# A graph-attention and hypergraph kernel: the order of the first three pairs

## The chip, the core and the metric

The kernel runs on one core of a Trainium2 chip. A core has a matrix engine (TensorE, PE in the profile), three engines for element work (VectorE or DVE, ScalarE or ACT, GpSimd or POOL) and a queue engine (SyncE or SP) that issues transfers. All of them run their own instruction streams in order and wait for each other by semaphores. SBUF is the working memory with 128 partitions; PSUM, in eight banks of 512 floats per partition, is where TensorE writes. The metric is the device time of one execution in microseconds; lower is better.

## The reference

`x` has 128 graphs of 128 nodes with 512 features, `adj` a 0/1 matrix for each graph. Layer 0 is graph attention with 8 heads of 64 units, then a residual and a layer norm. Layer 1 is two hypergraph convolutions with a ReLU and a layer norm between them, then two residuals and a layer norm. All is float32.

```python
# layer 0, per graph
feats = einsum('nf,hfu->hnu', X, W)
e_self, e_neigh = feats @ a_self, feats @ a_neigh            # per head and node
dense = leaky_relu(e_self[:, :, None] + e_neigh[:, None, :], 0.2)
dense = dense + -1e10 * (1 - A)
att = softmax(dense, axis=-1)
x = layernorm(x + relu(einsum('hij,hju->ihu', att, feats) + b))
# layer 1, per graph; hypergraph_conv(x, W) is
H = (adj != 0); w = adj[0]                                   # w: the first row
Dn = 1 / sum_e(H * w); Be = 1 / sum_n(H)
conv = Dn * (H @ (Be * (H.T @ (x @ W.T)))) + b
h = layer_norm(relu(conv(x, W1, b1)), gamma, beta)           # 512 -> 1024
y = conv(h, W2, b2) + x                                      # 1024 -> 512
out = layernorm(x + y)
```

## The kernel before, in words

The graphs are handled in 64 pairs. A pair passes through some five stages, and the stages of successive pairs overlap as in a pipeline. The program is written out without loops on the chip: every piece of work is a Python function, and `todo` holds each with a due time (`T` = 38.6 per pair and lag). Sorting by due time gives the order of the instructions on every engine's stream. The table `first` (L1161) gives single pieces of single pairs another due time; only the first pairs are in it. The times set an order and nothing else.

Stages of a pair, with the lines of the profile:

- Loads: `a` and the first row `w` (L106, L112), the rows `x` (L120), the rows in blocks `xb` (L129), the adjacency in blocks `ab` (L137). From pair 2 on, `x_transpose` (L385) turns `xb` on VectorE into `xT`; pairs 0 and 1 are turned on TensorE (L397).
- `nodes` (L360 to L369) makes the node degrees on VectorE; they go out to memory and come back spread over the partitions (`write_nodes`, `spread_nodes`, L374, L576). `edges` (L421 to L428) makes the edge degrees, `scale_edges` (L435) scales by them, `propagator` (`pd`) multiplies them and `r_evict` (L451) makes `R`, the propagation matrix.
- Features: for pairs 0 and 1 plain products (L523); from pair 2 on, seven half-size products in the manner of Strassen (`pfX`, `pfY`, `pfW`), with sums of operands on GpSimd (`x_sums`, L469), copies on ScalarE (L344) and sums of results on VectorE (`f_sum`, L509). The same seven products stand for the first weights (`ph`) and the second (`py`); `y_sum` (L935) adds the latter's results.
- Scores: `spread_rows` (L542) writes the per-node terms to memory, `neighbours` (L570) loads them to all partitions as `nb`. In four groups (two graphs, two halves of the heads): `masked` adds the mask (GpSimd, L589), `leaky` is the leaky ReLU with the own term (ScalarE, L605; one group of pair 0 on VectorE, L598), `largest` the maximum (VectorE, L611), `exponential` (ScalarE, L619).
- The exponentials must stand the other way round. For pair 0 TensorE turns them (L651). From pair 1 on they are written to memory (L623), read back in blocks (L631) and turned on VectorE in blocks (L640) into `eT`.
- Attention: products with `eT` (`pav`; L677 for pair 0, L703 for others, where the last head of both graphs shares a third bank), division (`attended`, L714, L735), residual and moments (L751, L759), reciprocal deviation (`rsa` on GpSimd from `vea`, L765 to L767), scaling on ScalarE (L794).
- Layer 1: `propagate` (`pz`), its copy (L829) and sums (L840), the hidden products, sums (L866), ReLU (L881), squares (L892), their tree of sums (`squares`, GpSimd, L904). For all but the last pairs the sums cross the partitions by a trip through memory: `sum_blocks` (L950 to L955), `write_sums` (L960), `read_sums` (L965), `sum_rest` (L973). From them `rsh` (L1002) and the scaling `y_scale` (L1006), then the output product `pq`, the last norm and the store.

The weights are prepared while the first pairs run: the attention vectors are folded into W0 (L230 to L238); `prepare_hidden` (L249) makes sums of W1 blocks; `prepare_output` (L276) multiplies gamma and beta through W2, its row sums are copied (L284) and spread (`gw`, `bw`, L288), and `prepare_output_blocks` (L300) rescales W2 by them in 16 instructions, after which the block sums follow (L226).

PSUM banks come in turn from one ring of eight. Transfers go out on SP's queue in program order, and a few early ones on ScalarE's; a transfer also waits until the one issued eight earlier on the same semaphore has landed.

Of the kernel before, what the change touches and what calls it, by code (L numbers as in the profile page):

```python
# [20 lines left out]
def kernel(  # L21
# [167 lines left out]
    load_adj(1)  # L189
# [61 lines left out]
    gbs = const.tile([P, KH, 2], F32, name="gbs")  # L251
# [13 lines left out]
    def prepare_rows():  # L265

        made["sel"] = work.tile([2, 2, P], F32, tag="zT", name="sel")
        nc.gpsimd.tensor_copy(
            made["sel"], ident[:2, :2].unsqueeze(2).to_broadcast([2, 2, P])
        )  # L270

    def prepare_output():
        pv = made["pv"] = [bank(f"pv{j}") for j in range(2)]
        for blk, i, j in w2_blocks:
            for k in range(KH // 2):
                nc.tensor.matmul(  # L276
                    pv[j][:2, :QU], gbs[:, i * KH // 2 + k, :], blk[:, k, :],
                    start=(i == 0 and k == 0), stop=(i == 1 and k == KH // 2 - 1),
                )

    def prepare_output_sums():
        made["sums"] = const.tile([2, F], F32, name="sums")
        for j in range(2):
            nc.vector.tensor_copy(made["sums"][:, j * QU:(j + 1) * QU], made["pv"][j][:2, :QU])  # L284
# [41 lines left out]
    def chain(kind, lag, times, multiply, w, extra=0, since=0, until=PAIRS):  # L326

        tag = "chain" if w == HALF else "half"

        def product(p, s, i):
            where, start = {1: ("X", 1), 2: ("Y", 1), 6: ("X", 0), 5: ("W", 1), 7: ("X", 0),
                            4: ("X", 0), 3: ("W", 0)}[i]
            if start:
                s[kind, where] = bank(f"{kind}{where}_{p}")
            multiply(s, i, s[kind, where], start)

        def copy(p, s, i):
            n = w + (extra if i < 2 else 0)
            t = s[kind, i] = work.tile([P, HALF if w == HALF else FW], F32, tag=f"{tag}_{i}", name=f"{kind}{i}_{p}")
            nc.scalar.copy(t[:, :n], s[kind, "X"][:, :n])  # L344

        for i, t in zip((1, 2, 6, 5, 7, 4, 3), times):
            at(lag, t, product, i, since=since, until=until)
        for i, t in enumerate(times[7:]):
            at(lag, t, copy, i, since=since, until=until)
# [166 lines left out]
    def plain_features(p, s, i):  # L516
        if i == 0:
            s["pf"] = [[bank(f"pf_{p}_{g}{j}") for j in range(2)] for g in range(2)]
        for j in range(2):
            w = (w0_sb[:, 0], w0_12, w0_sb[:, 1], w0_sb[:, 2])[2 * i + j]  # L520
            for g in range(2):
                for k in range(KF // 2):
                    nc.tensor.matmul(  # L523
                        s["pf"][g][j][:, :FW], s["xT"][:, g, i * KF // 2 + k, :],
                        w[:, k].rearrange("p h u -> p (h u)"), start=(i == 0 and k == 0),
                        stop=(i == 1 and k == KF // 2 - 1), skip_group_check=True,
                    )

    def plain_features_out(p, s):
        s["ft"] = fts[p]  # L530
        for j in range(2):
            for g in range(2):
                (nc.vector.tensor_copy if g or p else nc.scalar.copy)(  # L533
                    s["ft"][:, g, j * HH:(j + 1) * HH, :UW], by_head(s["pf"][g][j])
                )

    @step(1, 25.0)
    def spread_rows(p, s):


        rows = work.tile([P, B], F32, tag="rows", name=f"rows_{p}")
        nc.vector.transpose(  # L542
            rows.rearrange("p (c x) -> p c x", c=2),
            s["ft"][:, :, :, :2].rearrange("p g h c -> p c (g h)"),
        )
        shape = [B, NB, B] if p == 0 else [NB, B, B]
        rd = s["rd"] = dram.tile(shape, F32, tag="rd", name=f"rd_{p}")
        if p == 0:
            for b in range(NB):
                (nc.sync, nc.scalar)[b % 2].dma_start(rd[:, b, :], rows[b * B:(b + 1) * B])  # L550
        else:
            nc.sync.dma_start(rd.rearrange("b c j -> (b c) j"), rows)

    def blocked(p, t):

        dims = "p (h b j) -> p b h j" if p == 0 else "p (b h j) -> p b h j"
        return t.rearrange(dims, b=NB, h=H)

    @step(1, 27.0)
    def neighbours(p, s):  # L560
        s["nb"] = work.tile([P, 2, H * N], F32, tag="nb", name=f"nb_{p}")
        for g in range(2):
            dst, src, hs = s["nb"][:, g, :], s["rd"], slice((2 + g) * H, (3 + g) * H)
            if p == 0:
# [80 lines left out]
    def e_transpose_first(p, s, g, q):  # L645
        if (g, q) == (0, 0):
            s["eT"] = work.tile([P, 2, H, N], F32, tag="eT", name=f"eT_{p}")
        t = bank(f"pet_{g}{q}")
        for h in range(HH):
            n = (q * HH + h) * N  # L650
            nc.tensor.transpose(t[:, h * N:(h + 1) * N], s["nb"][:, g, n:n + N], ident)  # L651
        (nc.scalar.copy if q else nc.vector.tensor_copy)(
# [3 lines left out]
    for (g, q), tm, (lag, tl), (lagx, tx), te, tt in (  # L656
# [7 lines left out]
        at(2, tt, e_transpose, g, q, since=1)  # L664

    for g in range(2):
        at(2, (6.2, 10.9)[g], e_write, g, since=1)
        at(2, (10.0, 14.9)[g], e_read, g, since=1)
# [19 lines left out]
    @step(2, 20.9, since=1, until=LAST)  # L688
    def attend_rest(p, s):
        s["pav", 2] = bank(f"pav_{p}_2")  # L690

    @step(2, 24.1, since=1, until=LAST)
    def attend_pair(p, s):

        rest = s["pav", 2][:, :2 * (U + 1)].rearrange("p (g u) -> p g u", g=2)
        to = [(rest[:, g, :], g, HB) for g in range(2)]
        for g in range(2):
            t = s["pav", g] = bank(f"pav_{p}_{g}")
            to += [(t[:, h * (U + 1):(h + 1) * (U + 1)], g, h) for h in range(HB)]
        for t, g, h in to:  # L700
# [23 lines left out]
    def attended_pair(p, s):  # L724
# [4 lines left out]
        for r, t, dst in [(rden[:, :, HB], rest, heads[:, :, HB, :])] + [  # L729
# [3 lines left out]
        ]:  # L733
# [388 lines left out]
    for t, fn, *args in (  # L1122
# [17 lines left out]
        (12.1, load_weights, (nc.scalar, w2_blocks, w2t, DH // 2, QU)),  # L1140
        (13.05, prepare_vectors, ()),
        (14.05, load_weights, (nc.scalar, w1_blocks[:2], w1t, F // 2, HALF)),
        (12.95, load_first_row, (1,)),
        (15.46, load_weights, (nc.sync, w1_blocks[:1:-1], w1t, F // 2, HALF)),
        (16.1, everywhere, (b2_bc, b2, nc.sync)),
        (79.0, prepare_hidden, (nc.gpsimd, 0)), (79.1, prepare_hidden, (nc.gpsimd, 1)),
        (120.7, prepare_hidden, (nc.gpsimd, 2)), (110.6, prepare_hidden, (nc.vector, 3)),
        (15.5, prepare_output_vectors, ()), (16.0, prepare_output, ()),
        (78.3, prepare_rows, ()), (78.79, prepare_output_sums, ()),
        (78.99, prepare_output_spread, (0, "gw")), (98.0, prepare_output_spread, (1, "bw")),  # L1150
        (98.1, prepare_output_bias, ()), (98.2, prepare_output_blocks, (slice(0, 1),)),
        (99.75, prepare_output_blocks, (slice(1, 2),)),
        (117.8, prepare_output_blocks, (slice(2, 3),)),
        (118.1, prepare_output_blocks, (slice(3, 4),)),
        (126.5, prepare_output_block_sums, (nc.gpsimd, slice(0, 2))),
        (126.57, prepare_output_block_sums, (nc.vector, slice(2, 3))),
        (141.0, prepare_output_block_sums, (nc.vector, slice(3, 4))),
# [3 lines left out]
    first = {  # L1161
        ("spread_rows", 0): 13.5, ("neighbours", 0): 14.0,
        ("nodes", 0): 12.9, ("write_nodes", 0): 12.92, ("spread_nodes", 0): 15.9,
        ("edges", 0): 14.46, ("edges", 2): 119.2,
        ("x_transpose", 2, 0): 120.5, ("x_transpose", 2, 1): 121.1, ("scale_edges", 0): 14.47, ("propagator", 0): 14.55,
        ("r_evict", 0): 97.845,
        ("spread_rows", 1): 15.72, ("nodes", 1): 15.55, ("write_nodes", 1): 15.85,
        ("edges", 1): 110.4, ("scale_edges", 1): 110.5, ("neighbours", 1): 80.1,
        ("propagator", 1): 121.7, ("spread_nodes", 1): 80.3, ("r_evict", 1): 121.8,
        ("leaky", 0, 1, 1): 77.65, ("leaky", 0, 0, 1): 73.6, ("largest", 0, 0, 1): 75.3,  # L1170
# [4 lines left out]
        ("leaky", 1, 0, 0): 113.0, ("leaky", 1, 0, 1): 117.9, ("leaky", 1, 1, 0): 119.9,  # L1175
        ("largest", 1, 0, 0): 113.1, ("largest", 1, 0, 1): 118.2, ("largest", 1, 1, 0): 120.2,
        ("masked", 1, 0, 0): 98.0, ("masked", 1, 0, 1): 98.1, ("masked", 1, 1, 0): 98.2, ("masked", 1, 1, 1): 120.65,
        ("exponential", 1, 0, 0): 119.85, ("exponential", 1, 1, 1): 126.6,
        ("square", 0, 0, 0): 134.5, ("square", 0, 0, 1): 134.6,
        ("mask", 3): 152.0, ("sum_blocks", 0): 149.75, ("write_sums", 0): 149.76,  # L1180
        ("read_sums", 0): 149.77,
        ("squares", 0, 0, 0): 141.3, ("squares", 0, 0, 1): 141.4, ("squares", 0, 0, 2): 141.5,
        ("nodes", 2): 149.8, ("write_nodes", 2): 149.9, ("spread_nodes", 2): 150.3,
        ("r_evict", 2): 160.4,
        ("nodes", 3): 154.6, ("write_nodes", 3): 154.7, ("skip", 0): 132.5,
# [5 lines left out]
    for p, time, fn, *args in (  # L1191
# [3 lines left out]
        (0, 13.0, plain_features_out), (1, 13.1, x_transpose_out, 0), (1, 13.8, x_transpose_out, 1),  # L1195
        (1, 14.5, plain_features, 0), (1, 14.6, plain_features, 1),
        (1, 15.6, plain_features_out), (1, 97.9, adj_transpose_first),
        (0, 78.8, e_transpose_first, 0, 0), (0, 78.85, e_transpose_first, 0, 1),
        (0, 78.9, e_transpose_first, 1, 0), (0, 78.93, e_transpose_first, 1, 1),
    ):  # L1200
        todo.append((time, run, (fn, p, args)))
    for p in range(PAIRS):
        if p > 1:
            todo.append(({2: 79.5, 3: 143.1}.get(p, p * T), load, (p,)))
            todo.append((16.2 if p == 2 else p * T + (19.0 if p == 3 else 2.0), load_blocks, (p,)))
            todo.append((p * T + (28.5 if p == 2 else 20.5), load_edges, (p,)))
        for lag, time, name, pairs, fn, args in steps:
# [11 lines left out]
            if p == LAST - 1:  # L1219
                time = {  # L1220
                    ("product", 2): 24.22 if (lag, time) > (3, 20.0) else time,
                    ("product", 5): 29.5 if (lag, time) > (3, 20.0) else time,
# [53 lines left out]
```

## Time and profile before

| | us |
|---|---|
| median of 3 runs | 2405.86 (2405.43 to 2407.07) |
| the profiled execution | 2395.3 |
| its span | 2393.4 |
| mean granted TensorE clock | 0.996 |

The profile is of one execution. Its rows show one engine each: start, duration, engine, line, operation, result<-operands, shapes, count, and in brackets how long the engine was idle before and what ended that. Busy times of TensorE overlap, since products are pipelined: the step from one start to the next is what a product costs. Waits are put down to the releaser that came last.

Stretch by stretch, busy times in us:

| stretch | PE | DVE | ACT | POOL |
|---|---|---|---|---|
| 0 to 50 | 37.05 | 34.81 | 20.66 | 24.93 |
| 50 to 100 | 45.21 | 48.74 | 31.50 | 41.54 |
| 100 to 155 | 52.66 | 48.14 | 35.04 | 40.17 |
| 155 to 210 | 55.00 | 45.92 | 34.34 | 43.75 |

### The profile page before, as it was taken

Reading aid. Unit: us, or ns where it says so; the run is one execution under the profiler, and the core shown is the slowest. Engines: PE = TensorE matmul, PEld = TensorE weight load, DVE = VectorE, ACT = ScalarE, POOL = GpSimd, SP = SyncE. Lnnn points to the kernel's source line nnn. Section 1 sums busy time; section 2 is a strip of 40 time slices with the busy share of each in tenths; the row PEclk is TensorE's granted clock in tenths of the full one; section 3 lists DMA queues with packets and bytes.
Section 4 is the critical chain, followed back from the end, with each engine's and each line's share of the span. In section 5 each row is a group of like instructions: output and inputs, shape, how many; then the busy total and the mean of one; then the engine's idle time right before and its main releaser. Section 6 shows DMA issues by size and latency. Waiting matters only on the chain.

```text
span 2393.4 us, 80729 instructions
## 1 busy us (share of the span) xinstructions
PE 2360.8 (99%) x32309; PEld 2026.8 (85%) x32309; DVE 2089.6 (87%) x4456; ACT 1528.5 (64%) x4481; POOL 1825.6 (76%) x2060
## 2 busy tenths in 40 slices
PE   7899999999999999999999999999999999999998
PEld 6788887888888888888888888888888888888886
DVE  7989888898898898898898888988988988988975
ACT  4565765756667667667667666666676676676662
POOL 5877786777877877877877778778778778778774
PEclk9999999999999999999999999999999999999999
DMA  6555454555554555555545555544545555555541
GB/s 197 133 148 150 143 144 134 159 143 147 151 148 144 149 148 148 151 143 154 144 142 157 141 147 155 146 146 147 150 143 153 147 150 139 148 156 140 149 128 37
DMA packets 431134, 347.09 MB, mean 145 GB/s; under 512 B 151440, under 2 KB 380328, under 8 KB 430760
## 3 DMA queue, kind: packets, MB, share of 16 engines
q1 hardware_dynamic: 427288, 337.46, 49.5%
q8 instruction: 256, 4.19, 0.7%
q10 hardware_dynamic: 3472, 4.47, 0.6%
q14 instruction: 118, 0.97, 0.2%
HBM read 239.08 MB, written 102.73 MB: 143 GB/s over the span
## 4 chain that ended last, share of the span: by engine, by line
PE 89%; DMA 4%; DVE 3%; ACT 1%; POOL 1%; issue 1%; SPq 1%; DVEq 0%; POOLq 0%; ACTq 0%
PE phX L97 17%; PE pyX L97 17%; PE pfX L97 8%; PE pyW L97 8%; PE phW L97 8%; PE pav L703 5%; PE phY L97 4%; PE pz L97 4%; PE pfW L97 4%; PE pq L97 4%; PE pyY L97 4%; PE pfY L97 2%; DMA ed<-nb 1%; PE pd L97 1%; DMA nb<-rd 1%
## 5 line engine op out<-in xcount | busy, mean ns | idle before, releaser
L344 ACT COPY py<-pyX 128x257 f32<-128x257 f32 x189 | 70.7, 374 | 538.5 <-PE pyX L97 465.6
L97 PEld LDWEIGHTS phX<-zS,w_sb 128*64 128x64 f32 x6144 | 350.6, 137 | 36.3 <-POOL ft L742 23.1
L97 PE MATMUL phX<-zS,w_sb 128*64 128x128 f32 x6144 | 373.4, 273 | 2.6 <-ACT ph L344 2.6
L904 POOL TENSOR_TENSOR sq<-sq 128x512 f32<-128x512 f32 (+2 forms) x384 | 343.9, 896 | 20.1
L589 POOL TENSOR_TENSOR nb<-nb,neg 128x512 f32<-128x512 f32 x256 | 319.9, 1284 | 23.1 <-DMA nb<-rd 12.7
L605 ACT ACTIVATE nb<-nb,ft 128x128 f32<-128x128 f32 x1020 | 325.1, 392 | 13.7 <-POOL nb L589 13.7
L619 ACT ACTIVATE nb<-nb,nm 128x128 f32<-128x128 f32 x1024 | 319.4, 392 | 4.2 <-DVE nm L611 4.0
L767 POOL TENSOR_TENSOR rso<-veo,mhalf 128x2 f32<-128x2 f32 x63 | 44.2, 701 | 338.4 <-DVE veo L765 338.4
L97 PE MATMUL pyX<-w_sb,hS 128*64 128x257 f32 x2016 | 245.1, 380 | 0.0
L97 PE MATMUL pyX<-w_sb,h 128*64 128x257 f32 x2016 | 243.7, 379 | 0.5 <-ACT py L344 0.5
L97 PE MATMUL pyW<-w_sb,hS 128*64 128x256 f32 x2016 | 243.3, 378 | 0.0
L881 ACT ACTIVATE h<-h,vecs 128x128 f32<-128x128 f32 x768 | 239.4, 394 | 2.0 <-DVE h L866 1.4
L611 DVE TENSOR_REDUCE nm<-nb 128x4 f32<-128x512 f32 x256 | 175.2, 684 | 48.8 <-ACT nb L605 46.2
L97 PEld LDWEIGHTS pyX<-w_sb,h 128*64 128x64 f32 x2016 | 173.7, 136 | 46.2 <-ACT py L344 0.9
L97 PEld LDWEIGHTS pyW<-w_sb,hS 128*64 128x64 f32 x2016 | 174.7, 136 | 43.6 <-issue 0.3
L742 POOL TENSOR_TENSOR ft<-ft,b_bc 128x512 f32<-128x512 f32 x128 | 203.9, 1613 | 6.1 <-ACT ft L533 6.1
L97 PEld LDWEIGHTS pyX<-w_sb,hS 128*64 128x64 f32 x2016 | 168.7, 137 | 38.7 <-issue 0.8
L640 DVE STREAM_TRANSPOSE eT<-eb 128x512 f32<-128x512 f32 x252 | 163.5, 685 | 5.7 <-DMA eb<-ed 4.7
L805 DVE SCALAR_TENSOR_TENSOR o<-y,b_bc 128x512 f32<-128x512 f32 x128 | 164.7, 1325 | 0.0
L1006 DVE SCALAR_TENSOR_TENSOR y<-y,rsh,bw_bc 128x512 f32<-128x512 f32 x126 | 150.1, 1229 | 14.9 <-POOL rsh L1002 14.9
L469 POOL TENSOR_TENSOR hS<-h 128x512 f32<-128x512 f32 x126 | 162.1, 1287 | 0.0
L892 ACT ACTIVATE sq<-h 128x512 f32<-128x512 f32 x256 | 160.6, 629 | 2.1
(178 smaller groups left out, 5672.4 us busy)
## 6 DMA issues: line engine op xcount, KB each, us to landing
nb<-rd SPq DMA_DIRECT2D x127, 512.0 KB, 5.6
ed<-nb SPq DMA_DIRECT2D x126, 512.0 KB, 3.4
eb<-ed SPq DMA_DIRECT2D x504, 128.0 KB, 2.9
x<-in_x_dram SPq DMA_DIRECT2D x64, 512.0 KB, 4.0
out_dram<-o SPq DMA_DIRECT2D x63, 512.0 KB, 2.9
xb<-in_x_dram SPq DMA_DIRECT2D x248, 128.0 KB, 5.5
a<-in_adj_dram SPq DMA_DIRECT2D x64, 128.0 KB, 2.4
w<-in_adj_dram SPq DMA_DIRECT2D x128, 64.0 KB, 5.0
```

What stands on the lines that cost most here:

```text
L97: nc.tensor.matmul(to[rows], lhs[:, rows], rhs, start=start, stop=stop, skip_group_check=True)
L469: engine.tensor_tensor(t[:, i], in0, in1, op=op)
L589: nc.gpsimd.tensor_tensor(t, t, neg[:, :, None, :].to_broadcast([P, NB, HH, B]), op=ALU.add)
L605: nc.scalar.activation(t, t, AF.Prelu, bias=s["ft"][:, g, h, 0:1], alpha=SLOPE)
L611: nc.vector.tensor_reduce(s["nm"][:, g, hs], scores(p, s, g, hs).rearrange("p b h j -> p h b j"), AX.XY, ALU.max, negate=True,)
L619: nc.scalar.activation(t, t, AF.Exp, bias=s["nm"][:, g, h:h + 1])
L640: nc.vector.transpose(s["eT"][:, g, hs, :].rearrange("p h (b i) -> p h b i", b=NB), s["eb", g][:, :, hs, :].rearrange("p b h j -> p h b j"),)
L742: nc.gpsimd.tensor_tensor(t, t, b0_bc.rearrange("p (h u) -> p h u", h=H), op=ALU.add)
L805: nc.vector.scalar_tensor_tensor(s["o"][:, g, :], s["y"][:, g, :], 2.0, b2_bc, op0=ALU.mult, op1=ALU.add)
L881: nc.scalar.activation(dst[:, k, :], src[:, k, :], AF.Relu, bias=b1_sb[:, c:c + 1])
L892: nc.scalar.activation(s["sq"][:, g, q * KH // 2:(q + 1) * KH // 2, :], hid(s, g, q), AF.Square, scale=DH ** -0.5,)
L904: nc.gpsimd.tensor_tensor(t[:, :n, :], t[:, :n, :], t[:, n:2 * n, :], op=ALU.add)
```

## The change

Due times of pairs 0 to 3 are moved, and some pieces are done in another way:

- Pair 2's features run around pair 0's propagation: five products before it and two after it. Its rows are loaded and turned early, and its row terms are sent early.
- Pair 1's exponentials are turned on TensorE, as pair 0's; their trip through memory is dropped, and pair 1's score terms lie head by head as pair 0's.
- For pair 0, leaky comes ahead of the mask.
- In `attend_pair` the heads run in order (graph 0, graph 1, each with its last head at its end), and `attended_pair` reads in that order.
- Pair 1's plain features run one half of the columns after the other.
- `prepare_output` makes 32 result rows at a time in one bank in place of 2 rows in two banks; the sums are then copied and spread over 128 partitions.
- Loads are regrouped: two of four W2 blocks and pair 1's adjacency go behind pair 0's neighbour terms, pair 1's first rows far later.
- Nodes, edges, squares, sums and preparations of the first pairs stand elsewhere in the queues.

```diff
-    load_adj(1)
-    gbs = const.tile([P, KH, 2], F32, name="gbs")
+    gbs = work.tile([P, KH, B], F32, tag="y", name="gbs")
+    nc.gpsimd.memset(gbs, 0.0)
+    one = small.tile([P, 2], F32, tag="one", name="one", bufs=1)
+    nc.vector.tensor_reduce(
+        one, ident.rearrange("p (c r) -> p r c", c=NB)[:, :2], AX.X, ALU.add
+    )
...
     def prepare_output():
-        pv = made["pv"] = [bank(f"pv{j}") for j in range(2)]
...
+        t = made["pv"] = bank("pv")
+        for n in range(2):
+            for j in range(2):
+                for c in range(NB):
+                    k = 2 * c + n
+                    blk = w2_blocks[2 * (k // (KH // 2)) + j][0]
+                    nc.tensor.matmul(
+                        t[c * B:(c + 1) * B, j * QU:(j + 1) * QU], gbs[:, k, :],
+                        blk[:, k % (KH // 2), :], start=(n == 0 and j == 0), stop=(n == 1),
+                        skip_group_check=True,
+                    )
...
-        at(2, tt, e_transpose, g, q, since=1)
+        at(2, tt, e_transpose, g, q, since=2)
...
-        at(2, (6.2, 10.9)[g], e_write, g, since=1)
-        at(2, (10.0, 14.9)[g], e_read, g, since=1)
+        at(2, (6.2, 10.9)[g], e_write, g, since=2)
+        at(2, (10.0, 14.9)[g], e_read, g, since=2)
...
     def attend_rest(p, s):
-        s["pav", 2] = bank(f"pav_{p}_2")
+        s["pav", 0] = bank(f"pav_{p}_0")
...
+        s["pav", 1], s["pav", 2] = (bank(f"pav_{p}_{g}") for g in (1, 2))
         rest = s["pav", 2][:, :2 * (U + 1)].rearrange("p (g u) -> p g u", g=2)
-        to = [(rest[:, g, :], g, HB) for g in range(2)]
+        to = []
         for g in range(2):
-            t = s["pav", g] = bank(f"pav_{p}_{g}")
+            t = s["pav", g]
             to += [(t[:, h * (U + 1):(h + 1) * (U + 1)], g, h) for h in range(HB)]
+            to.append((rest[:, g, :], g, HB))
...
-        (12.1, load_weights, (nc.scalar, w2_blocks, w2t, DH // 2, QU)),
+        (12.1, load_weights, (nc.scalar, w2_blocks[:2], w2t, DH // 2, QU)),
+        (14.03, load_weights, (nc.sync, w2_blocks[2:3], w2t, DH // 2, QU)),
+        (14.04, load_weights, (nc.scalar, w2_blocks[3:], w2t, DH // 2, QU)),
+        (14.045, load_adj, (1,)),
-        (12.95, load_first_row, (1,)),
+        (80.2, load_first_row, (1,)),
...
+        ("edges", 3): 157.0,
+        ("write_nodes", 3): 158.6,
+        ("nodes", 3): 158.5,
+        ("nodes", 2): 144.25,
+        ("read_sums", 0): 152.22,
+        ("sum_blocks", 0): 152.2,
+        ("squares", 0, 1, 2): 151.5,
+        ("squares", 0, 1, 1): 151.4,
+        ("squares", 0, 1, 0): 151.3,
+        ("nodes", 1): 121.72,
+        ("x_transpose", 2, 1): 78.1,
+        ("x_transpose", 2, 0): 75.4,
+        ("leaky", 0, 1, 1): 15.61,
+        ("leaky", 0, 1, 0): 69.62,
+        ("leaky", 0, 0, 1): 69.61,
+        ("leaky", 0, 0, 0): 69.6,
+        ("edges", 2): 144.21, ("scale_edges", 2): 144.22,
+        ("pf_product", 2, 1): 78.991, ("pf_copy", 2, 0): 78.9915, ("pf_product", 2, 2): 78.992,
+        ("r_evict", 1): 144.23,
...
+        (1, 124.95, e_transpose_first, 0, 0), (1, 124.96, e_transpose_first, 0, 1),
+        (1, 130.41, e_transpose_first, 1, 0), (1, 130.42, e_transpose_first, 1, 1),
...
-            todo.append((16.2 if p == 2 else p * T + (19.0 if p == 3 else 2.0), load_blocks, (p,)))
-            todo.append((p * T + (28.5 if p == 2 else 20.5), load_edges, (p,)))
+            todo.append(({2: 11.05, 3: 105.8}.get(p, p * T + 2.0), load_blocks, (p,)))
+            todo.append(({2: 105.7, 3: 146.85}.get(p, p * T + 20.5), load_edges, (p,)))
```

## The prediction

> **What bounds the kernel now.** I read the busy times of the page first, then TensorE's waits, then each engine's timeline of the first 170 us.
>
> ```profile
> PE 2360.8 (99%) x32309; PEld 2026.8 (85%) x32309; DVE 2089.6 (87%) x4456; ACT 1528.5 (64%) x4481; POOL 1825.6 (76%) x2060
> ```
>
> TensorE is busy nearly all the time. Its timeline far into the run shows one pair's propagation start and the next's:
>
> ```profile
> 1008.67 1.95 PE L97 MATMUL pz<-R,y 128*64 128x128 f32 x32
> ...
> 1045.04 1.95 PE L97 MATMUL pz<-R,y 128*64 128x128 f32 x32
> ```
>
> A pair costs 36.37 us, with no gap between rows. So from about 155 us to the tail only TensorE counts, and a change to the first pairs moves the end by what it moves TensorE's arrival there. TensorE's waits, longest in total first (us, times, longest):
>
> ```profile
> PE px L397 <- DMA x<-in_x_dram: 8.1, 1, 8.1
> PE pz L97 <- ACT y L794: 4.0, 1, 4.0
> PE pav L703 <- DVE eT L640: 4.0, 2, 2.3
> PE phX L97 <- ACT ph L344: 2.6, 2, 1.9
> PE phX L97 <- ACT zT L829: 1.3, 2, 0.9
> PE pfX L97 <- ACT pf L344: 1.2, 2, 0.7
> ```
>
> Past the first load, about 11 us of gaps lie in the start-up. Its landmarks, from the TensorE timeline (start, duration, and in brackets the gap before):
>
> ```profile
> 29.72 1.89 PE L276 MATMUL pv<-w_sb,gbs 128*2 128x256 f32 x8
> ...
> 47.23 3.68 PE L97 MATMUL pz<-R,y 128*64 128x128 f32 x32 [4.05 <-ACT y L794]
> ...
> 87.06 1.94 PE L97 MATMUL pz<-R,y 128*64 128x128 f32 x32
> ...
> 101.26 1.92 PE L97 MATMUL pq<-y,R 128*64 128x512 f32 x8
> ...
> 116.62 1.97 PE L703 MATMUL pav<-ft,eT 128*64 128x65 f32 x60 [1.72 <-DVE eT L640]
> ```
>
> Pair 0's propagation starts at 47.23, pair 1's at 87.06, pair 2's attention products end at 118.59. Busy time by stretch says what bounds the stretch: VectorE was busy 48.7 of 50 us from 50 to 100, TensorE 45.2. The start-up is bound by VectorE, in queue order. VectorE's timeline shows pair 2's node degrees stretched:
>
> ```profile
> 86.63 1.36 DVE L360 SCALAR_TENSOR_TENSOR w<-a,w 128x128 f32<-128x128 f32 x1
> ...
> 88.03 1.12 DVE L365 TENSOR_SCALAR dn<-dd 128x2 f32<-128x2 f32 x1
> ...
> 105.08 0.28 DVE L360 SCALAR_TENSOR_TENSOR w<-a,w 128x128 f32<-128x128 f32 x1
> ```
>
> The set took 4.4 us beside GpSimd's masks (86.14 to 90.54), 1.35 us with GpSimd idle (105.08). Last, the sync queue: the round trip of the square sums, and the write of pair 2's exponentials.
>
> ```profile
> 86.24 0.33 SPq L960 DMA_DIRECT2D sd<-sr  x1
> 89.41 0.63 SPq L965 DMA_DIRECT2D sums_out<-sd  x1
> ...
> 98.68 1.43 SPq L623 DMA_DIRECT2D ed<-nb  x1
> ```
>
> **What the Trainium skill says.** "SBUF — State Buffer", Who interferes with whom: a VectorE instruction with two SBUF inputs, or in a two-port mode, and a GpSimd instruction that reads SBUF block each other for the whole instruction. The 4.4 against 1.35 us agrees. "TensorE: Matmul & The Clock Gate", What's actually happening: after some 3.4 us idle the array runs at half rate. Agrees: after the 4.05 us gap, propagation took 3.46 us start to start (47.23 to 50.69), pair 1's 1.75. "TensorEngine Tiling (Array Packing)", Theoretical Speedup: products of 32 output columns can run up to four at once. The trace shows two at once for 64 columns (a 264-wide record takes 0.11 us of TensorE, 8 in 0.89, against 0.233 at full width, 16 in 3.73), not four. "DMA: Bandwidth & Descriptors", Anatomy of one DMA: about 2 us fixed. The square sums' write took some 3.1 us here (86.24 to 89.41).
>
> **The change, part by part,** in times of this execution.
>
> *To pair 0's normalization.* Before, ScalarE starts at 29.24, after the first mask, and runs 3.73 + 4.77 us without a hole to 37.64. With leaky first it starts at the landing, 27.95: leaky to 31.7, masks behind it (1.27 each) to 34.2, exponentials 31.7 to 36.65, held 0.2 by a maximum that stands behind a turn of pair 2's rows (1.06). That is 1.0 us; with the transposes and copies of that step, vea comes at 44.0 instead of 45.16. The weight product pv is 32 records of 256 columns: 7.0 us now, 1.7 if four run at once. Two W2 blocks now load behind pair 0's neighbour rows. Those and W1 moved 3.2 MB from 24 to 35.7, 273 GB/s, so the blocks land near 31.5, pv ends near 33.3, before the transposes need TensorE. If not four at once, pv ends at 38.5 and all that follows is 1.5 to 2 us later. The last W1 block lands 1.2 MB / 273 = 4.2 us later, near 39.9; behind it on SP stand pair 1's row writes and neighbour loads, which land near 45, as now (no engine waited for them at 45.92). Cover about 1 us.
>
> *The gap at 43.18.* Pair 2's features, 7 x 0.89 us, move here from 64.9 to 74.4; four and a fifth fill 40 to 45.4. Propagation starts near 45.9, at full rate, ends 47.7 instead of 50.7; two more products follow, and the hidden layer starts at 49.5 instead of 50.69. Later TensorE no longer spends 6.2 us plus 1.2 us of gaps on these, but 1.9 us on pair 1's transposes and 0.9 on bw. Its own bound for pair 1's propagation is then 82, 5 us earlier than 87.06.
>
> *VectorE's queue.* Same operations, other order. From vea_0 44.0: a hold of 2.3 us, because the second feature sum stands behind the ScalarE copy that follows y (46.95); then by their spacing in this trace 0.7 + 6.3 (16 W2 rescales at 0.39) + 2.4 (maxima) + 1.1 + 1.8 (hidden sums) + 1.4 (nodes of pair 1, out of 25.7) + 1.5 (edges) + 2.6 (four PSUM copies for four turns of 0.65) + 1.3 + 0.5 + 1.8 + 0.2 = 21.6, to 67.9. Contended: half of the 3 us seen for nodes, 0.9 for the rest; waits for pair 1's last leaky and hidden sum, 1.1: 71.4. Attended to vea_1 takes 5.9 (78.51 to 84.42): 77.3. Before: 84.4.
>
> *What is late next.* Between vea_1 and the y sum that frees pyW now stand: a W2 sum 1.06, edges of pair 2 2.0, its scaling 0.5, R 0.33, nodes 1.36. That is 5.3 us clear, 11.3 at the worst this trace shows for each (2.15, 2.5, 1.9, 0.33, 4.4); GpSimd's masks and squares run just then, so I take 8.3. The two sums, 0.7: 86.3. The last weighing product (1.7) is queued behind them: pair 1's propagation at 88.0, against 87.06. The 5 us are spent: +0.9, bounds -2 and +4.
>
> *To pair 2's attention.* GpSimd's second squares move behind the masks: ready near 87. A turn, a maximum and the block sums on VectorE (1.05, 0.6, 1.0): 89.0. The round trip (sd issue to readable, 5.7 us from 86.24 and 89.41 plus a like landing) ends at 94.7, and VectorE now stands waiting there some 3 us; before, it came at 96.18 without a wait. Behind it: sums 0.5, maximum 0.6, edges 1.9, nodes 2.9, so 100.6. Then h sum, two scalings and R, 2.9: output product at 103.5 (101.26 before). SP writes pair 2's exponentials after those nodes: 101.1 (98.68 before). The chain from that write to the turned second group took 16.5 us before (115.17), so 117.6. TensorE gets there at 103.5 + 13.2 (101.26 to 114.58, less its gaps) + 0.7 for ScalarE's copy = 117.4. With heads in order, group 0 (0.95 us) runs while group 1 is turned, to 118.35: end 119.4 against 118.59, +0.8. The same order covers pair 3's 0.62 gap. Sum: +0.2 us on 2395.3, 2395.5. The runs shown have a median 10.6 us above the profiled execution; the difference carries over: 2406.
>
> *At nothing:* heads in order past pair 3 (same 60 + 4 records; TensorE has no gap there), later loads of pairs 2 and 3 (each lands 10 us or more before its reader), one sum copy for two, the constant `one` (a small reduction ahead of the folded weights, which end at 15.65 and are first read at 16.42), gbs's memset (GpSimd idle until 6.04). Pair 2's rows: four issues of 0.3 to 0.56 on SP, ahead of pair 0's node and row writes of 17.0 and 21.0, done by 13. Pair 1's first rows, moved behind its neighbour loads: two issues near 41, read near 58.
>
> **Rivals.** *Faster:* clear runs at the low ends. Then vea_1 is 76, the y sums 82.5, the square sums 91, the write near 96.5, and attention ends near 114.3: 4.3 + 0.6 + up to 3 if the wait for the sums is shorter, so -5 to -8 us, 2399. For it: in steady state the same instructions run clear. Against: GpSimd's masks start right after vea_1.
>
> *Slower:* one mechanism, VectorE stopped at the read of the square sums. Everything of pair 2 and 3 is queued behind it; a trip of 9 instead of 5.7 us (the sync queue has waited 4.2 us for the write alone), or squares 3 us later, moves write and output product equally. It decides from about 4.5 us late: +5 to +9, 2412.
>
> *The change does not do what it says:* four-at-once fails, or two holes around pv halve TensorE's rate. Costs 1.5 to 3 us at 40, part absorbed: stays inside the likeliest.
>
> **How the numbers follow.** Likeliest, the trade, 0.55: 2406, own range 2402 to 2410. Faster rival 0.25, slower 0.20. Changes under 0.2% (4.8 us) are about what a measurement of this kernel cannot tell from none. The range 2398 to 2412 leaves out about 0.1 on each side.
>
> **What would show it.** Right: propagation of pair 0 near 46 and at full rate; no gap of 4 us before it; pv in 1.7 us; vea_1 near 77; TensorE waiting for the y sum before the last pyW; VectorE idle 2 us or more before L985; the write of pair 2's exponentials near 101; steady 36.37 us a pair. Wrong: pair 1's propagation by 83, or any gap past 160 us.

## The result and the profile after

The changed kernel is slower: 2420.18 us median (2416.46 to 2423.54) against 2405.43 (2400.35 to 2407.07) for the kernel before, five runs each, a ratio of 1.007 (95% interval 1.0057 to 1.0084), some 15 us. The forecast was 2406, within 2398 to 2412. The profiled execution of the changed kernel took 2421.44 us, span 2419.6, at a mean granted clock of 0.995.

Engines' busy times, as the page has them:

```profile
PE 2366.7 (98%) x32325; PEld 1910.7 (79%) x32325; DVE 2081.2 (86%) x4456; ACT 1528.5 (63%) x4481; POOL 1819.8 (75%) x2061
```

TensorE has hardly more work, and 16 records more of products and 16 of weight loads. What grew is its waiting. Its waits (us, times, longest):

```profile
PE phX L97 <- ACT zT L841: 15.2, 19, 1.7
PE px L404 <- DMA x<-in_x_dram: 8.0, 1, 8.0
PE pyW L97 <- DVE y L947: 4.5, 1, 4.5
PE pq L97 <- DVE y L1018: 3.6, 2, 3.0
PE pav L715 <- DVE eT L648: 3.2, 6, 0.8
PE pv L282 <- DMA w_sb<-in_w2t_dram: 2.7, 1, 2.7
PE phW L97 <- DVE h L878: 2.3, 1, 2.3
```

The first row is new: 19 waits for the copy of the propagated rows, all past 200 us, where the forecast had TensorE without a gap. The start-up on TensorE's timeline, the rows that answer to those shown of before:

```profile
34.44 1.08 PE L282 MATMUL pv<-w_sb,gbs 128*32 128x256 f32 x4
...
47.09 1.97 PE L97 MATMUL pz<-R,y 128*64 128x128 f32 x32 [1.48 <-ACT y L806]
...
89.54 3.68 PE L97 MATMUL pyW<-w_sb,hS 128*64 128x256 f32 x16 [4.51 <-DVE y L947]
92.98 2.50 PE L97 MATMUL pz<-R,y 128*64 128x128 f32 x32
...
107.68 3.63 PE L97 MATMUL pq<-y,R 128*64 128x512 f32 x8 [3.04 <-DVE y L1018]
...
122.58 2.07 PE L715 MATMUL pav<-ft,eT 128*64 128x65 f32 x64
```

Pair 0's propagation is level with before (47.09 against 47.23), pair 1's is 5.92 us late (92.98 against 87.06), pair 2's (134.85) 6.06, pair 3's (171.22 against 166.00) 5.22. VectorE's rows for pair 2's node factors, and pair 4's for comparison:

```profile
84.80 1.35 DVE L367 SCALAR_TENSOR_TENSOR w<-a,w 128x128 f32<-128x128 f32 x1
...
86.19 1.11 DVE L372 TENSOR_SCALAR dn<-dd 128x2 f32<-128x2 f32 x1
...
98.70 0.45 DVE L985 STREAM_TRANSPOSE so<-sums_out 128x256 f32<-128x256 f32 x1 [4.58 <-DMA sums_out<-sd]
...
110.94 0.28 DVE L367 SCALAR_TENSOR_TENSOR w<-a,w 128x128 f32<-128x128 f32 x1
```

The factors still meet GpSimd's masks (83.42 to 88.49 here), now ahead of the y sums, and VectorE then stands 4.58 us at the square sums. The sync queue's side of it:

```profile
92.90 0.74 SPq L972 DMA_DIRECT2D sd<-sr  x1
96.65 0.63 SPq L977 DMA_DIRECT2D sums_out<-sd  x1
...
105.59 0.37 SPq L631 DMA_DIRECT2D ed<-nb  x1
```

**Where the 26 us between the two profiled executions lie.** 5.22 us are there when pair 3's propagation starts. From there to the start of pair 62's, 59 periods, the kernel before takes 2151.89 us and the changed one 2173.06: 21.2 us more. The tail is equal (from the last propagation to the end of the span 40.1 us both times). At 36.37 us a period (from one propagation's start to the next), 59 periods are 2145.8: so the kernel before also lost 6.1 us here, which the prediction had not seen, and the changed kernel 27.2. The medians lie 15 us apart, not 26, since the profiled execution of the kernel before was 10 us under its median.

Propagation starts of the changed kernel on TensorE, first in a bad stretch, then in a good one:

```profile
690.00 1.92 PE L97 MATMUL pz<-R,y 128*64 128x128 f32 x32
...
693.81 1.97 PE L97 MATMUL phX<-zT,w_sb 128*64 128x128 f32 x32 [1.46 <-ACT zT L841]
...
728.05 1.92 PE L97 MATMUL pz<-R,y 128*64 128x128 f32 x32
...
1397.13 1.91 PE L97 MATMUL pz<-R,y 128*64 128x128 f32 x32
...
1433.51 1.91 PE L97 MATMUL pz<-R,y 128*64 128x128 f32 x32
```

38.05 us against 36.38. Periods of 36.5 to 38.3 us are frequent up to period 33 (counted by the pair whose propagation opens it) and rare after.

**What is late in a bad period.** On the sync queue, the write of a pair's row terms and the neighbour load that waits for it; a bad period, then a good one:

```profile
678.78 0.39 SPq L560 DMA_DIRECT2D rd<-rows  x1
681.97 0.94 SPq L578 DMA_DIRECT2D nb<-rd  x2
...
1422.24 0.34 SPq L560 DMA_DIRECT2D rd<-rows  x1
1423.69 1.75 SPq L578 DMA_DIRECT2D nb<-rd  x2
```

The neighbour load can be issued 3.19 us after the write, 16 KB, in one case and 1.45 in the other. GpSimd's mask then starts at 689.27, 0.73 us ahead of the next propagation, and not 2.63 ahead (1430.88). ScalarE has two groups of leaky queued ahead of the copy zT, so zT starts 3.20 us after the propagation (693.20) and not 1.32 (1434.83), and TensorE waits 1.46 us.

Call a write late when the neighbour load comes over 1.95 us behind it. In this execution 32 of 59 are late, and 27.0 of the 27.2 us lost stand in the periods that follow a late write. In the profiled execution of the kernel before 12 of 59 are late, and 6.0 of its 6.1 us stand behind them.

**Why the write is late.** The transfer view over 2 us of the bad case (679.4 to 681.4, 0.05 us a figure), and over 1.5 us of the good one (1422.2 to 1423.7, 0.0375 us a figure):

```profile
GB/s 87 123 97 79 57 67 131 431 59 18 8 0 0 0 0 0 0 0 0 0 0 0 0 0 0 5 5 8 8 8 8 8 10 3 0 0 0 0 0 0
q8 instruction: 1, 0.02, 2.9%
```

```profile
GB/s 79 79 75 82 92 96 75 55 51 34 41 41 62 85 58 89 119 120 120 96 92 82 34 10 89 120 89 75 48 14 0 0 0 0 0 0 0 0 437 0
q8 instruction: 1, 0.02, 5.8%
```

One packet of the queue "instruction" starts in each, the spike of 431 and 437 GB/s. In the bad case it starts at 679.75, in the midst of the write. Most of what was in flight is through by 679.95; then 0.7 us with nothing, and from 680.65 to 681.1 the rest trickles, some 3 KB (the last nine figures add up to 63 GB/s, each over 0.05 us). The packet's duration in the trace is 0.92 us, so the rest moves when the packet is done. In the good case the packet starts at 1423.63, 0.3 us after the last of the other bytes.

The landing signals say how much is held. The trace has sixteen for each transfer, as many as the page counts DMA engines. Of the bad write's, fifteen come from 680.13 to 680.30 and the sixteenth at 681.96; the load issued just before it has fifteen by 680.09 and its last at 681.78. In the good case all sixteen of the write come within 0.17 us. So it is in 31 of the 32 late writes of the changed kernel and in all 12 of the kernel before: a single signal is over 0.4 us behind the rest. This fits one DMA engine that the packet holds, with its share of the other transfers queued behind.

The page counts 256 such packets with 4.19 MB, 16 KB each, four for each pair. The Trainium skill ("Runtime: NRT & Kernel Launch", Instruction fetch mechanics) says what they are: an engine's instructions come in blocks of 16 KiB, 256 instructions, by a DMA queue of its own. The trace agrees, and shows whose they are: it has 65,573 instructions of TensorE, which is 256 times 256 and 37 more. The page calls their cost mostly hidden; here it is not.

**The arithmetic of the phase.** The phase is the place in the period at which a fetch falls. A period has 504 products, 504 weight loads and 14 semaphore waits on TensorE in the trace: 1022 instructions, two short of four blocks. So each fetch comes two instructions later in every period, and its place drifts past the write. The change adds 36 instructions ahead of the steady state (16 transposes for pair 1's exponentials, a load and a product each, and four waits). 36 / 2 = 18 periods: a place that the kernel before reaches in period 14, the changed one reaches in period 32. Late writes end in period 14 in the one and in period 32 in the other, but for a few single ones.

### The profile page after: what moved, and what is told of

It is laid out like the page before. It is cut to its first block, busy times and chain, and to the rows that moved or that the text cites. A ratio compares the mean times of both kernels' runs of the same rounds, so it can differ in the third digit from the quotient of the medians.

```text
span 2419.6 us, 80749 instructions
## 1 busy us (share of the span) xinstructions
PE 2366.7 (98%) x32325; PEld 1910.7 (79%) x32325; DVE 2081.2 (86%) x4456; ACT 1528.5 (63%) x4481; POOL 1819.8 (75%) x2061
## 3 DMA queue, kind: packets, MB, share of 16 engines
q8 instruction: 256, 4.19, 0.7%
## 4 chain that ended last, share of the span: by engine, by line
PE 62%; DMA 18%; ACT 5%; DVE 5%; POOL 4%; SPq 2%; issue 2%; DVEq 0%; POOLq 0%
PE phX L97 12%; PE pyX L97 11%; DMA ed<-nb 7%; PE phW L97 6%; PE pfX L97 6%; DMA nb<-rd 6%; PE pyW L97 6%; PE phY L97 3%; PE pq L97 3%; PE pfW L97 3%; PE pav L715 3%; PE pz L97 3%; DMA rd<-rows 3%; PE pyY L97 3%; ACT nb L613 2%; DMA eb<-ed 2%
## 5 line engine op out<-in xcount | busy, mean ns | idle before, releaser
L97 PEld LDWEIGHTS pyW<-w_sb,hS 128*64 128x64 f32 x2016 | 152.1, 137 | 72.2 <-issue 6.5
L97 PEld LDWEIGHTS pyX<-w_sb,h 128*64 128x64 f32 x2016 | 151.8, 137 | 68.0 <-ACT py L350 0.9
L97 PEld LDWEIGHTS pyX<-w_sb,hS 128*64 128x64 f32 x2016 | 146.5, 137 | 59.7 <-POOL hS L476 1.0
```

Of the source, the lines that this page charges most:

```text
L97: nc.tensor.matmul(to[rows], lhs[:, rows], rhs, start=start, stop=stop, skip_group_check=True)
```

## The experiments

*Theory.* The steady loss comes from the phase of TensorE's instruction fetch against the transfers, which the change shifts by 36 instructions; the start-up adds its 5 us through VectorE's order. *Rivals:* heads in order, which is in every pair, costs the steady state; or a start-up that ends late leaves the queues behind for thirty pairs.

The phase can be moved alone: products of 2 by 2 numbers into a bank that is overwritten next, while TensorE waits for its first rows. Each is four instructions. All ratios are to the kernel before, run beside them on the same chip.

**Heads in order alone** (`e1_heads`): the kernel before with these edits of the change.

```diff
-        s["pav", 2] = bank(f"pav_{p}_2")
+        s["pav", 0] = bank(f"pav_{p}_0")
...
+        s["pav", 1], s["pav", 2] = (bank(f"pav_{p}_{g}") for g in (1, 2))
...
-        to = [(rest[:, g, :], g, HB) for g in range(2)]
+        to = []
...
+            to.append((rest[:, g, :], g, HB))
```

> The kernel before with one part of the change: attention heads in order (the banks, the products and the reads of every pair from 1 to 62). TensorE's instruction count is that of before. Rival (heads in order cost the steady state): pairs of 37 to 38 us as in the changed kernel until about pair 33, some 10 us slower, about 2415. Theory (the phase of TensorE's instruction fetch against the neighbour rows' write costs it): same fetch phase as before, so 2405 within 3 us, slow pairs up to about pair 15 only.

Measured: 2398.88 us, ratio 0.9977 (0.9965 to 0.999), where no change was forecast. Late writes end in period 15. The rival is out: heads in order doesn't slow the steady state. Pair 3's propagation came at 164.73 us, 1.3 sooner; where the rest of the small gain comes from was not found, and it does not come back in the padded kernels below (0.9973 with heads in order, 0.9971 without).

**36 instructions and nothing else** (`e2_pad36`):

```diff
         s["px"] = [bank(f"px_{p}_{g}") for g in range(2)]
+        for _ in range(9 if p == 0 else 0):
+            nc.tensor.matmul(s["px"][0][:2, :2], mhalf, mhalf, start=True, stop=True)
```

> The kernel before with nine 2x2 products on TensorE ahead of the first transposes, while it waits for the first rows: 36 more TensorE instructions, as many as the change adds, and nothing else. Theory (fetch phase): the start-up is untouched (pair 3's propagation at 166 us), but each fetch falls where it fell 18 pairs sooner, so the slow pairs last to about pair 33 instead of 15: 8 to 15 us slower, 2413 to 2420. Rivals (heads in order, or a start-up that ends late): no difference, 2405.

Measured: 2421.49 us, ratio 1.007 (1.005 to 1.009): 17 us slower by the ratio, 19 by the medians, a little more than forecast. Pair 3's propagation stands at 166.17, as in the kernel before; late writes last to period 34 (29 of 59 writes, 12 in the kernel before). TensorE's waits in it:

```profile
PE pav L705 <- DVE eT L642: 18.4, 14, 2.2
PE phX L97 <- ACT zT L831: 8.6, 12, 2.0
```

Nine tiny products at a time when TensorE has nothing to do cost as much as the whole change. Here most of the loss shows at the attention products, with the old order of heads; in the changed kernel it shows at the copy zT.

**The changed kernel with one whole fetch added** (`e3_after_pad220`): 55 products, the same edit in the changed kernel.

> The changed kernel with 55 such 2x2 products, 220 TensorE instructions: with the 36 of the change that makes 256, one whole fetch, so the fetches fall as in the kernel before. Theory (fetch phase): slow pairs end near pair 15, the time falls by 8 to 15 us to about 2410, and what is left over before is the start-up's 5 us. Rivals (heads in order, late start-up): 2420 as the changed kernel.

Measured: 2408.3 us, ratio 1.0016 (1.0005 to 1.0027). Late writes end in period 14, as in the kernel before. With that kernel's phase the change costs 0.16%, 4 us (1 to 6 by the interval), and not 0.7%. In the profiled execution, 5 us above this median, pair 3's propagation was later than expected (176.56, against 171.22 with the same order of work); why is not known.

**A better phase for the kernel before** (`e4_pad228`): 57 products.

> The kernel before with 57 such products, 228 instructions, which is 28 fewer than one whole fetch: each fetch falls where it fell 14 pairs later. Theory (fetch phase): the slow pairs 4 to 15 of the kernel before are gone or end by pair 3, so it beats the kernel before by 6 to 12 us, about 2395. Rivals: 2405.

Measured: 2396.3 us, ratio 0.9971 (0.9957 to 0.9985), 6 us faster, with the late writes at the front gone. The same write and load in the run with 36 instructions, then in this one:

```profile
229.20 0.34 SPq L554 DMA_DIRECT2D rd<-rows  x1
231.82 0.94 SPq L572 DMA_DIRECT2D nb<-rd  x2
```

```profile
228.35 0.34 SPq L554 DMA_DIRECT2D rd<-rows  x1
229.89 1.62 SPq L572 DMA_DIRECT2D nb<-rd  x2
```

2.62 us against 1.54. In periods 56 to 60 another of the four fetches comes to the write: five late ones at the end, and the periods behind them lose 1.9 us. Another 4.5 us are lost in periods 30, 49, 50 and 54, which follow no late write; TensorE waits there for attention operands, and what held these was not looked into.

**The start-up: the y sums alone** (`e5_nodes_back`): the changed kernel, with

```diff
-        ("write_nodes", 2): 144.26,
-        ("nodes", 2): 144.25,
+        ("write_nodes", 2): 152.26,
+        ("nodes", 2): 152.25,
...
-        ("edges", 0): 14.46, ("edges", 2): 144.21, ("scale_edges", 2): 144.22,
+        ("edges", 0): 14.46, ("edges", 2): 152.23, ("scale_edges", 2): 152.24,
...
-        ("spread_nodes", 2): 150.3,
+        ("spread_nodes", 2): 152.3,
```

> The changed kernel with pair 2's degrees, edges and node factors (and their writes and reads) moved back behind the y sums and the block sums on VectorE, as the kernel before has them. Theory (the y sums stood 8.3 us behind pair 1's normalization, and that wait cost TensorE a cold restart): pair 1's propagation starts near 87 to 88 instead of 92.98, without the 4.5 us wait; the round trip of the square sums still ends near 98, now covered by the degrees, so the output product stays near 107 and pair 3's propagation comes 1 to 3 us sooner than 171.2. Rival (GpSimd's masks, not this order, hold VectorE): pair 1's propagation stays past 91. The time is not read from this run: its fetch phase is the changed kernel's.

One execution took 2404.49 us. Its rows:

```profile
87.50 1.94 PE L97 MATMUL pz<-R,y 128*64 128x128 f32 x32
94.99 1.28 PE L97 MATMUL pd<-hT,hB 128*64 128x128 f32 x8 [5.55 <-DVE hB L442]
...
107.91 1.94 PE L97 MATMUL pq<-y,R 128*64 128x512 f32 x8 [1.58 <-DVE y L1018]
```

Pair 1's propagation gains 5.48 us, and the rival about GpSimd's masks is out for this wait. But the output product stays at 107.91, and pair 3's propagation comes at 170.42, 0.8 sooner where 1 to 3 were forecast: the gap only moves, to the product of pair 2's edges. The y sums were late, yet they did not set the end of the start-up. The rows point to the squares: GpSimd still takes them behind the masks, VectorE waits 3.68 us for them, and their sums go out at 95.32. No run moved the squares alone.

**The front of the change with the old tail** (`e8_tail_pad192`): the changed kernel with the order of before for the squares, sums and degrees, and 48 products (229 instructions with the change's own).

```diff
-        ("write_nodes", 3): 158.6,
-        ("nodes", 3): 158.5,
-        ("write_nodes", 2): 144.26,
-        ("nodes", 2): 144.25,
-        ("read_sums", 0): 152.22,
-        ("write_sums", 0): 152.21,
-        ("sum_blocks", 0): 152.2,
-        ("squares", 0, 1, 2): 151.5,
...
+        ("write_nodes", 3): 154.7,
+        ("nodes", 3): 154.6,
+        ("write_nodes", 2): 149.9,
+        ("nodes", 2): 149.8,
+        ("read_sums", 0): 149.77,
+        ("write_sums", 0): 149.76,
+        ("sum_blocks", 0): 149.75,
+        ("squares", 0, 1, 2): 144.4,
...
-        ("edges", 0): 14.46, ("edges", 2): 144.21, ("scale_edges", 2): 144.22,
+        ("edges", 0): 14.46, ("edges", 2): 149.79, ("scale_edges", 2): 149.795,
```

> The changed kernel with pair 2's degrees and edges, the second squares, the block sums and pair 3's node factors put back in the order of before, and 48 of the 2x2 products (192 instructions; with the change's own 37 the fetches fall nearly as in the padded kernel before). Theory: the front part of the change (pair 0's normalization, features moved ahead, pair 1's turns) then keeps its gain: pair 1's propagation near 87 to 88, the output product near 101 to 103, pair 3's propagation at 163 to 166, no slow pairs: 2388 to 2396. Rival (the front part itself costs): pair 3's propagation stays past 168 and the time above 2400.

Measured: 2391.25 us, ratio 0.998 (0.9972 to 0.9988).

```profile
86.56 1.94 PE L97 MATMUL pz<-R,y 128*64 128x128 f32 x32
...
102.48 1.94 PE L97 MATMUL pq<-y,R 128*64 128x512 f32 x8 [1.82 <-DVE y L1020]
```

Pair 3's propagation is at 165.80, 5.4 us sooner than in the changed kernel and level with the kernel before (166.00). The tail here is the order of degrees, squares and sums at the end of the start-up. So the start-up's loss is that of the tail, and the front of the change (pair 0's normalization, features ahead, pair 1's turns) brings next to nothing that arrives there: 0.5 us against the old start-up with such products (166.33, next run). Which of the tail's pieces counts was not separated.

**The old start-up with heads in order and the good phase** (`e7_heads_pad228`): the edits of the first run and 57 products.

> The kernel before with heads in order and the 57 products of 228 instructions. If both gains are what they seem (start-up 1.3 us, fetch phase 6 us), they add: about 2392 to 2395, 0.3 to 0.5% under before. If heads in order gained by chance of the run: 2396.

Measured: 2390.44 us, ratio 0.9973 (0.9964 to 0.9982). It beats both kernels, as the one above does; between these two the intervals do not tell. The gains do not add: heads in order brings nothing that shows once the phase is good.

**The worst phase** (`e9_pad128`): the kernel before with 32 products, half a fetch.

> The kernel before with 32 of the 2x2 products, 128 instructions: half a fetch. Theory (fetch phase): in the padded runs the fetch that meets the neighbour rows' write from the front left it at a place reckoned as pair 15 of the kernel before, and the next one came into it at place 70; one fetch further round (128 places) the meeting so spans places -58 to 15, and 128 instructions put the pairs 3 to 62 on places -61 to -2, inside it from end to end. So nearly every pair is slow, by 0.4 to 1.2 us: 25 to 60 us slower, 2425 to 2460, with pair 3's propagation still at 165 to 167. Rival (it is the number of added products or the start-up they disturb that counts, not the phase): between the runs with 9 and with 57 products, within 10 us of the kernel before.

Measured: 2417.58 us, ratio 1.0087 (1.0069 to 1.0105), 21 us slower, pair 3's propagation at 165.02. The rival is out: 32 products cost 21 us where 57 gain 6. 56 of 59 writes are late, from period 6 to the last. The forecast of 25 was just missed: the loss for each late write is about 0.5 us here and 1.2 in the run with 36 instructions. In periods 6 to 25, where another of the fetches falls some 7 us after each propagation, it is 0.3 us a period; from 48 on, where one falls mostly 0.9 to 1.7 us after it as in the bad stretch of the other runs, it is 0.9. Which transfer that second fetch meets was not separated. The trace has a candidate: the write of a pair's second half of exponentials, 512 KB. From its issue to that of the next read it took 4.77 us (median of 50) when a fetch began between 0.5 us before and 3 us after, and 3.65 otherwise (median of 9).

**The change with the good phase** (`e10_after_pad192`): 48 products in the changed kernel.

> The changed kernel with 48 of the products (192 instructions): the fetch phase of the fast padded runs, the whole change otherwise. Theory: no slow pairs, and what remains against the padded kernel before is the start-up alone, 5 to 10 us: pair 3's propagation at 171 to 176, the time 1.000 of the kernel before (0.998 to 1.002), some 5 to 10 us above the padded kernel before with heads in order. Rival (the rest of the change costs the steady state too): above 1.004.

Measured: 2397.47 us, ratio 1.0005 (0.9996 to 1.0015). Pair 3's propagation is at 169.71. The late writes at the front are gone (eight are left, five of them in periods 56 to 60), and against the kernel with old start-up, heads in order and the same phase the change costs 7 us by the medians. At pair 3's propagation 3.4 us of it are there (169.71 against 166.33); this profiled execution was 3.7 us under its median, and the rest is not placed. Against the run with the old tail, which has the same 48 products and differs in that order alone, it is 6.2 us by the medians and 3.9 at pair 3's propagation: with the phase held, the tail is what the change's start-up loses.

## Why the prediction was wrong

**"So from about 155 us to the tail only TensorE counts, and a change to the first pairs moves the end by what it moves TensorE's arrival there."** This step failed, and most of the 15 us with it. It was read from two rows at 1008 and 1045 us, in the calm part. The trace of before had its own bad stretch, here the worst period of it:

```profile
349.02 1.94 PE L97 MATMUL pz<-R,y 128*64 128x128 f32 x32
...
375.75 3.47 PE L703 MATMUL pav<-ft,eT 128*64 128x65 f32 x60 [2.32 <-DVE eT L640]
...
389.44 1.93 PE L97 MATMUL pz<-R,y 128*64 128x128 f32 x32
```

40.42 us, with the write of the period before 3.32 us long, and the wait list that was quoted held it ("4.0, 2, 2.3"): one of those two waits was put to the start-up without looking where the other stood. The test that the prediction set itself, "any gap past 160 us", came out against it.

**A term at nothing without a reason:** the place of instructions in TensorE's stream. The 16 transposes were priced by their time alone (1.9 us; they took 1.1 us twice), and neither the sum nor the list "At nothing" has a line for what they shift. The 36 instructions that came with them cost 17 to 19 us when as many were added alone.

**"To pair 2's attention ... Sum: +0.2 us."** Mis-sized: +5.22. The slower rival had the mechanism, VectorE stopped at the read of the square sums with the squares late, and its +5 to +9 holds the 5.22; it was given 0.20. Term by term:

| step | predicted | measured |
|---|---|---|
| pair 0's propagation starts, ends | 45.9, 47.7 | 47.09, 48.88 |
| pv | 1.7 us, four at once | 28 records from 32.26 to 35.44, two at once |
| vea_1 | 77.3 | 80.34 |
| from vea_1 to the end of the y sums | 9.0 | 9.05 |
| pair 1's propagation | 88.0 | 92.98 |
| squares ready | near 87 | 91.07 |
| trip of the square sums | 5.7 | 5.8 (92.90 to 98.70) |
| output product | 103.5 | 107.68 |
| pair 2's attention ends | 119.4 | 124.44 |

The queue prices held (the y sums, the trip). What failed first is vea_1, 3 us late: TensorE waited 2.34 us for a hidden sum ahead of pair 1's turns, and the next product ran at half rate (phW, 3.56 us start to start, 1.75 elsewhere), so the attention products came at 73.10 and VectorE at 74.13, not 71.4. From there masks, squares and sums are all late by 3 to 4 us. The other term missing is the same half rate behind the waits that came on TensorE: the last pyW took 3.44 us in place of 1.73, the propagation behind it 2.31 in place of 1.75, pq 3.35 in place of 1.72. The granted clock was 0.50 over that pyW, 0.53 over pq and over the phW, against 1.00 from 50.6 to 58. The prediction cited the clock gate and priced it where the change removes a wait and for holes around pv, not here. Its figure of some 3.4 us idle is not what these waits show: the phW and pq came after 2.34 and 3.04 us.

**Right:** pair 0's propagation at full rate, with a gap of 1.48 us in place of 4.05, though it starts only 0.14 us sooner; TensorE waiting for the y sum ahead of the last pyW; VectorE idle 2 us or more (4.58) before the sums; heads in order without cost past pair 3. The rate of pv did not matter: the exponentials end at 35.9, pv at 35.4.

**What stays open.** How much one late write costs ranges from 0.4 us (one execution of the run with the y sums moved, on a chip where the kernel before took 2396.6 us) to 1.2. So the split of the changed kernel's 15 us is by the runs: with the old phase it keeps 4 of them (1 to 6), the rest is phase. The start-up varies too: the same order of work brought pair 3's propagation at 169.71, 171.22 and 176.56 in three runs, so 5.22 is one execution's figure. That the late signal is of the very DMA engine that carries the fetch is read from the times; the trace does not number the engines, and no run moved the fetch to another.

## What to carry to other kernels

Count the period of the bounding engine over the whole run, not at one place; two calm rows prove nothing about the other sixty. In a kernel written out at length, an edit that adds or drops instructions shifts every later instruction fetch; before an edit of under 1% is judged, pad the stream to the same phase, or take several phases. Price a wait of over 2 us on TensorE with the slow product behind it, and follow each late result to the one that ends last: moving the y sums alone gained 5.5 us at pair 1 and 0.8 at pair 3.

## What was not expected of the hardware

- A TensorE instruction fetch is one 16 KB packet that mostly takes 0.9 to 1.5 us. A 16 KB write that meets one between 0.3 us before and 1.2 us after its issue takes 2.7 to 3.1 us in place of some 1.5 (medians of each run). In 31 of the changed kernel's 32 late writes a single one of sixteen landing signals was behind.
- With 1022 instructions a period, the meeting drifts by two instructions a period, so one start-up instruction more or less shifts a bad stretch by half a period. The same kernel ran from 0.9971 to 1.0087 of its time by tiny products in an idle stretch alone.
- Waits of 2.34 and 3.04 us on TensorE were enough for a granted clock of about half behind them.
- Products of 32 result rows ran two at once (0.114 us each at 256 columns, against 0.233 for one of 264 at full width), not four.
